# Half of the softmax maxima move from a matmul into eight biased exponentials, and small Newton steps move from VectorE to GpSimd, in a cross-attention and six-layer local-attention kernel

## The chip, the cores and the metric

The kernel runs on one core of a Trainium2 chip. A core has a matmul engine (TensorE, PE in the profile; its weight loads are listed apart as PEld), VectorE (DVE), ScalarE (ACT), GpSimd (POOL), a queue that only issues transfers (SyncE, SP), and DMA engines that carry them out. Each engine works through its own list of instructions in order and waits on semaphores where another engine's result is needed. The metric is the device time of one execution in microseconds; lower is better.

## The reference

The input is 32 sequences of 128 tokens of width 128. First comes one cross-attention block (16 heads of width 8, 4 key and value heads), then six layers that each hold a local attention and a feed-forward block. What matters here is the local attention of one layer:

```python
q, k, v = split(shift_tokens(x) @ Wqkv)            # 16 heads of width 64
q = q / max(norm(q), 1e-12) * q_scale              # the same for k
q, k = rotary(q), rotary(k)
# windows of 32 queries, each against its own and the window before it: 64 keys
sim  = einsum('bhwie,bhwje->bhwij', q, look(k)) * 8.0
sim  = where(mask, -big, sim)
attn = softmax(sim, -1)                            # a row of 64 keys
x    = (einsum('bhwij,bhwje->bhwie', attn, look(v))) @ Wo + x
```

The feed-forward block after it is a layer norm, two projections to 341 columns with a GELU gate, and a projection back. All of it is computed in fp32, with most weights split into a high and a low part for the fast fp32 format of TensorE.

## The kernel before, in words

The 32 sequences form 8 groups of 4. After the cross-attention (`xgroup`, `xunit`) the kernel loops over 6 layers and 8 groups, 48 times `lgroup`. Each calls `unit` four times, once per sequence, and then `ffn`. So there are 192 units, and nearly all of the time goes into them.

One unit, with the operation's name in the planner and its line in the profile:

- `qk` (L437 to L439): four projections of 512 columns, each as three matmuls; `sq` (L785, ACT) squares them, `ss` (L800, DVE) sums the squares per head; `tab` (L791, DVE) multiplies with the rotary tables; `add` (L797, POOL) adds the two rotary parts.
- `newton` turns the 32 sums of squares per token into inverse norms, exp(-0.5 ln v) and one Newton step. For the units' norms (`floor` is given) `dmx` (L395) clamps on VectorE, `ln` and `ep` (L398, L401) and the square `ysq` (L405) run on ScalarE, and two fused steps `dnw` (L411, L417) run on VectorE. For the layer norms (`eps` is given, 4 values per token) the same function runs on GpSimd in five small steps (L393, L407, L413, L419, L422).
- `mul` (L814, POOL) applies the inverse norms, `tq` (L443, PE) transposes, `evq` (L819, ACT) copies out of PSUM.
- `msk` (L856, ACT) writes the mask into the two score banks (bank 66 for the even heads, a = 0, bank 67 for the odd heads, a = 1); `sc` (L851, PE) adds the scores, 128 small matmuls.
- `soft(a)`, for each bank: `mx` (L864, DVE) takes minus the maximum of each of eight rows of 64 scores; `fold` (L865, PE) adds it to the scores in PSUM, a matmul of the identity with the maxima broadcast to 512 columns; `ex` (L867, ACT) is one exponential over 512 columns; `sm` and `rl` (L868, L869, DVE) sum and invert, `pl` (L870, POOL) normalizes, `pt` (L872, DVE) transposes in blocks of 32.
- `y`, `yt`, `dm` (L437 to L439, L832 ACT, L833 SP) make the values and move them with a transfer; `av` (L885, PE) sums over keys.

Each engine's order is not the program's order. Every operation is handed to a scheduler, `Sched`, with a priority (the unit's number plus an offset in the table `LATER`) and with costs in the table `COST` (engine, time on it, time until done). `Sched.run` plays these through and fixes the order in which the instructions are written for each engine; `KEEP` says how many PSUM banks of the five common ones an operation must leave free. The chip then follows that order, whatever its own durations are. Units overlap deeply: while the scores of unit u run, the projections of units u+3 and u+4 and the norms of u+2 are under way.

`ffn` per group: `res` (L893, DVE) adds the attention, `psh` (L750 and L751, SP) shifts tokens by a transfer, `st` (L899, DVE) takes statistics after it, `xn` (L913, ACT) normalizes in four pieces with a scale and a bias from SBUF, `gate` and `pa` (PE), `gel` (L930, ACT, with a bias from SBUF and a change of ScalarE's table before and after), `um` (DVE), `w2` (L949, PE).

Of the kernel before, what the change touches and what calls it, by code (L numbers as in the profile page):

```python
# [16 lines left out]
P = 128  # L17
# [4 lines left out]
GB = 4  # L22
TX = 0.44
NS = 4
NW = "dve"


COST = dict(
    ax=("PE", 0.4, 0.64), axh=("ACT", 0.52, 0.62), axl=("DVE", 0.6, 0.7),
    qk=("PE", 0.75, 0.95), sq=("ACT", 0.52, 0.62), ss=("DVE", .62, .72), tab=("DVE", 1.14, 1.22), add=("POOL", 1.28, 1.31), ta=("DVE", .63, .72), adda=("POOL", 1.1, 6),  # L30
    mxs=("POOL", .26, .30), dmx=("DVE", 0.4, 0.48), dnw=("DVE", 0.34, 0.42), ln=("ACT", .2, .24), ep=("ACT", .2, .24), nw=("POOL", .31, .34),
    mul=("POOL", 1.01, 1.06), tq=("PE", 0.44, 0.68), evq=("ACT", .5, .62), evk=("ACT", .5, .62),
    y=("PE", 0.75, 0.95), yt=("ACT", 0.52, 0.62), dm=("SP", 0.6, 8.0), xph=("ACT", .6, .7), xpl=("ACT", .6, .7), dw=("SP", .62, 3.5), dr=("SP", .62, 4.5),
    msk=("ACT", 0.54, 0.63), sc0=("PE", .52, .75), sc1=("PE", .52, .75), mx=("DVE", .62, .7), fold=("PE", 0.31, 0.5), ex=("ACT", .5, .62),
    sm=("DVE", .62, .7), rl=("DVE", .14, .22), pl=("POOL", 1.05, 1.07), pt=("DVE", .64, .74), av=("PE", 1.95, 2.15), sc=("PE", 1.42, 1.62),
    res=("DVE", .63, .72), psh=("SP", 1.65, 3.5), st=("DVE", 0.78, 0.86), ag=("DVE", .35, .40), xn1=("POOL", 1.08, 1.1),
    eps=("POOL", .22, .26), lnf=("ACT", .22, .21), epf=("ACT", .22, .21), nwf=("POOL", 0.18, 0.24), xn=("ACT", 1.55, 1.65), nmr=("DVE", 0.4, 0.48), ysq=("ACT", .2, .24), xn2=("POOL", 1.08, 1.1),
    ptn=("PE", .46, .70), xnh=("ACT", .51, .62), xnl=("DVE", .60, .66), gate=("PE", 0.75, 0.95), gel=("ACT", 0.63, 0.7),
    pa=("PE", 0.73, 0.94), um=("DVE", 0.68, 0.76), w2=("PE", .67, .90), res2=("DVE", .63, .72), xo=("POOL", 1.3, 1.3),
# [4 lines left out]
    xst=("DVE", 0.8, 0.87), xag=("DVE", .30, .35), xnw=("POOL", .20, .20), xtr=("PE", 0.52, 0.68), xev=("ACT", .49, .60),  # L44
    xpj=("PE", 0.98, 1.15), hil=("ACT", .58, .70), lof=("DVE", .66, .75), pv=("PE", .90, 1.1), vt=("DVE", .25, .30),
    td=("PE", .90, 1.1), abs=("ACT", .52, .65), lnb=("ACT", .55, .64), mkb=("DVE", .42, .42), tbm=("DVE", .95, 1.0),
    xsc=("PE", 0.38, 0.58), xmx=("DVE", .86, .95), xsb=("POOL", 1.10, 1.10), xex=("ACT", .55, .65), xpa=("PE", 1.1, 1.3),
    xrl=("DVE", 0.17, 0.25), xat=("DVE", .21, .29), pwm=("PE", .90, 1.1), xrs=("DVE", .63, .70),
)

LATER = dict(y=2.95, fold=4, xsc=-0.75, evk=-0.25, ss=0.5, sq=4.05, axl=-2.3, mul=1.5, mx=-0.75, evq1=0.1, tab0=-2.0,
    lnb=0.75, xpj=0.85, tab3=0.85, lnf=0.45, dmx=-0.5, xst=1.05, tq3=2.45, xat=0.7, pv=1.9, msk0=-2.15, sq2=-0.65,
    nw=1.5, pa2=-0.85, xex=3.7, lof=-0.25, ss1=1.1, xmx=-1.85, yt0=-1.3, mul3=0.55, io=-0.85, rl0=4.05, bip=-1.45,
    td=0.25, add3=4.1, gate0=-1.55, add0=-2.5, xnh=-0.95, ex1=-0.4, pa0=1.6, pl0=3.1, bid=3.5, ln=0.95, ss2=-0.75,
    sq0=0.25, sq1=0.35, xpa=0.25, qkl=3, mul0=-2, xn1=4.1, tq2=-0.25, mul1=1.45, xsb=1.7, w2=-2.0, sq3=0.5, ex=-0.5,
    wvp=-1.05, ax=-0.5, xtr=0.1, qk3=-1.65, qk=-0.7, evq0=0.65, qkh=1.0, w1b=-0.6, pl1=2.8, mh=3, yt3=0.5, gel2=-1.65,
    w1a=0.95, tab2=-0.25, ysq=-1.05, qk1=-2.15, res=2.2, xo=0.25, av=0.75, tq1=1.0, epf=-1.3, gate2=-1.75, pa1=4,
    tab=0.35, mx1=-0.5, sm0=1.85, pt0=-0.05, gel0=-1.05, ml=-1.5, ptn=2.1, ep=-2.75, sm1=-0.65, xrl=-1.4, um=1,
    add2=3, dm=-1, evq=0.45, tq0=1.3, nwf=3, yt1=-1.1, msk=-1.5, um2=-1.6, pwm=-0.2, w1c=0.1, mkb=0.95, gel=0.95,
    pt1=-0.75, wve=2.25, fold1=-0.75, gate=0.75, xnl=-0.1, dm3=-2.25, xn=4.2, yt2=-0.75, st=-0.5, xag=0.5, mul2=1.75,  # L60
    tb=-1, psh=-0.25, rl1=2.1, pl=1.75, yt=-0.75, evq3=1, dnw=-1, um1=0.45, sm=-0.25, abs=0.6, gate1=0.3, msk1=-0.05,
    dm0=0.6, gel1=-0.4, nmr=2.0, fold0=-2.5, axh=-0.75, y3=3.1, res2=2.75, dm2=0.5, vt=2, hil=-1.3, ss0=0.5, pa=1.5,
    eps=-1, dm1=0.45, xev=0.45, um0=-1, ag=0.75, tq=0.25)

KEEP = dict(qk=0, y=0, gate=1, pa=1, xtr=0, xpj=0, pv=1, td=1, xsc=1, wvp=2, mp=2, bip=2, sc0=0, tq=0, ptn=0, ax=0,
    w2=1)
LAT = dict(PE=.06, ACT=.05, DVE=.08, POOL=.16, SP=.08)


# [156 lines left out]
def body(ctx: ExitStack, tc: tile.TileContext, x, ctx_in, fside, mask_in, xWq, xWk, xWv, xWo, xtw,  # L226
         Wqkv, q_scale, k_scale, Wo, ln_g, ln_b, W1, b1, W2, b2, cst, x1d, out):
    nc = tc.nc
# [153 lines left out]
    def newton(names, pri, V, src, n, floor, eps, pool_, cols):  # L382
        v, y, t = [Buf(p) for p in pool_]

        def sl(b):
            return b.t[:, 0:n]

        small = NW == "dve" and floor is not None
        e = nc.vector if small else nc.gpsimd

        def f0():
            if eps is not None:
                e.tensor_scalar(sl(v), cols(), eps, None, op0=ALU.add)  # L393
            else:
                e.tensor_scalar(sl(v), cols(), floor, None, op0=ALU.max)  # L395

        def f1():
            nc.scalar.activation(sl(y), sl(v), AF.Ln)  # L398

        def f2():  # L400
            nc.scalar.activation(sl(y), sl(y), AF.Exp, scale=-0.5)  # L401

        def f3():
            if small:
                nc.scalar.activation(sl(t), sl(y), AF.Square)  # L405
            else:
                e.tensor_tensor(sl(t), sl(y), sl(y), op=ALU.mult)  # L407

        def f4():
            if small:  # L410
                e.scalar_tensor_tensor(sl(t), sl(v), -0.5, sl(t), op0=ALU.mult, op1=ALU.mult)  # L411
            else:
                e.tensor_tensor(sl(t), sl(t), sl(v), op=ALU.mult)  # L413

        def f5():
            if small:
                e.scalar_tensor_tensor(sl(y), sl(t), 1.5, sl(y), op0=ALU.add, op1=ALU.mult)  # L417
            else:
                e.tensor_scalar(sl(t), sl(t), -0.5, 1.5, op0=ALU.mult, op1=ALU.add)  # L419
# [6 lines left out]
        S.op("ysq" if small else names[3], f3, pri, [y], [t])  # L426
        S.op(names[3], f4, pri, [t, v], [t])
        if small:
            S.op(names[3], f5, pri, [y, t], [y])
        else:  # L430
            S.op(names[3], f5, pri, [t], [t])
            S.op(names[3], f6, pri, [y, t], [y])
        return y

    def split3(pt, lhs, rhs):
# [336 lines left out]
    def unit(l, g, j, w, G, pri):  # L772
# [29 lines left out]
            S.op("add", add, pri, [t], [rt], k=c)  # L802
        for c in range(4):
            proj(c)
        rn = newton(("dmx", "ln", "ep", "dnw") if NW == "dve" else ("mxs", "ln", "ep", "nw"), pri, None, ss, 32, 1e-24, None, ("rv", "ry", "rw"), lambda: ss.t)
        qT = []
        for c in range(4):
            def tr(c):
# [50 lines left out]
        def r8(b):  # L859
            return b.t.rearrange("p (a c) -> p a c", c=64)  # L860

        def soft(a):
            s, mx, pr, sm, PT = sc[a], Buf("mx"), Buf("pr"), Buf("sm"), PTs[a]
            S.op("mx", lambda: nc.vector.tensor_reduce(mx.t, r8(s), axis=AX.X, op=ALU.max, negate=True), pri, [s], [mx], k=a)  # L864
            S.op("fold", lambda: nc.tensor.matmul(s.t, identr, mx.t.unsqueeze(2).to_broadcast([P, 8, 64]), start=False,  # L865
                                                  stop=True, skip_group_check=True), pri, [mx, s], [s], k=a)
            S.op("ex", lambda: nc.scalar.activation(pr.t, s.t, AF.Exp), pri, [s], [pr], table="E", k=a)  # L867
# [168 lines left out]
```

## Time and profile before

| | |
|---|---|
| time, median of 3 runs | 3084.66 us (3080.82 to 3087.93) |
| the profiled execution's own time | 3085.37 us |
| its span, first to last instruction | 3083.6 us |
| mean granted TensorE clock | 0.987 |
| busy: PE, DVE, POOL, ACT | 96%, 90%, 78%, 76% of the span |
| instructions | 114504 |

A line of the profile names the source line, engine, operation, and output tile <- input tiles. "Busy" is the time in which at least one instruction of that engine ran, by the profile. The ends of matmuls are modelled and include the way into PSUM, so that two following matmuls overlap in the list; the distance from one start to the next says what a matmul costs on the engine. The windows view gives busy times per stretch with the number of instructions in brackets. The chain is the sequence of work that ended last, followed backwards from the end of the program.

### The profile page before, as it was taken

Reading aid. Unit: us, or ns where it says so; the run is one execution under the profiler, and the core shown is the slowest. Engines: PE = TensorE matmul, PEld = TensorE weight load, DVE = VectorE, ACT = ScalarE, POOL = GpSimd, SP = SyncE. Lnnn points to the kernel's source line nnn. Section 1 sums busy time; section 2 is a strip of 40 time slices with the busy share of each in tenths; the row PEclk is TensorE's granted clock in tenths of the full one; section 3 lists DMA queues with packets and bytes.
Section 4 is the critical chain, followed back from the end, with each engine's and each line's share of the span. In section 5 each row is a group of like instructions: output and inputs, shape, how many; then the busy total and the mean of one; then the engine's idle time right before and its main releaser. Section 6 shows DMA issues by size and latency. Waiting matters only on the chain.

```text
span 3083.6 us, 114504 instructions
## 1 busy us (share of the span) xinstructions
PE 2960.5 (96%) x47887; PEld 2337.7 (76%) x47887; DVE 2787.6 (90%) x5779; ACT 2335.2 (76%) x4799; POOL 2416.5 (78%) x2470
## 2 busy tenths in 40 slices
PE   8999999999999999999999999999999999999997
PEld 5666777787777777777777777777777787777785
DVE  5778999998999999999999999999999998999994
ACT  6877777777777777777777777777777877777774
POOL 6667978878878878878878878878788787778783
PEclk7999999999999999999999999999999999999998
DMA  4100645545544546544446544446545455445454
GB/s 111 32 17 22 102 74 82 89 74 94 95 75 79 89 78 104 92 76 82 85 76 105 90 79 83 80 80 106 87 77 87 74 89 92 78 88 88 83 92 67
DMA packets 216870, 250.70 MB, mean 81 GB/s; under 512 B 90622, under 2 KB 111394, under 8 KB 216354
## 3 DMA queue, kind: packets, MB, share of 16 engines
q1 hardware_dynamic: 215922, 243.04, 45.5%
q8 instruction: 377, 6.18, 1.1%
q14 instruction: 139, 1.14, 0.2%
q10 hardware_dynamic: 432, 0.34, 0.0%
HBM read 25.31 MB, written 4.19 MB: 10 GB/s over the span
## 4 chain that ended last, share of the span: by engine, by line
PE 55%; DVE 27%; ACT 7%; DMA 5%; issue 5%; SPq 1%; POOL 0%; DVEq 0%; POOLq 0%; ACTq 0%
PE bank__68 L885 8%; DMA xt<-xt 4%; PE bank__66 L851 2%; PE bank__65 L443 2%; PE bank__62 L443 2%; PE bank__64 L443 2%; PE bank__62 L949 2%; PE bank__63 L437 2%; PE bank__67 L851 2%; PE bank__65 L437 2%; PE bank__64 L437 2%; PE bank__61 L437 2%; PE bank__63 L443 2%; PE bank__63 L439 2%; PE bank__63 L438 2%
## 5 line engine op out<-in xcount | busy, mean ns | idle before, releaser
L856 ACT COPY bank__66<-mask 128x512 f32<-128x512 f32 x192 | 117.3, 611 | 4.7 <-PE bank__66 L361 4.7
L856 ACT COPY bank__67<-mask 128x512 f32<-128x512 f32 x192 | 115.5, 602 | 1.7 <-PE bank__67 L361 0.7
L244 ACT ACT_TABLE_LOAD x48 | 61.6, 1283 | 0.9
L930 ACT ACT_TABLE_LOAD x48 | 61.6, 1283 | 0.8
L722 ACT ACTIVATE ysh__88<-ysh__88 128x512 f32<-128x512 f32 x64 | 40.4, 640 | 5.1 <-POOL ysh__88 L720 4.9
L893 DVE TENSOR_TENSOR xt<-bank__68,xt 128x512 f32<-128x512 f32 x48 | 32.6, 679 | 1.2 <-PE bank__68 L885 1.2
L953 DVE TENSOR_TENSOR xt<-bank__62,xt 128x512 f32<-128x512 f32 x25 | 16.3, 653 | 2.8 <-PE bank__62 L949 2.8
L960 POOL TENSOR_TENSOR raw__49499<-raw__49499,xt 128x512 f32<-128x512 f32 x1 | 1.3, 1261 | 14.9 <-DVE xt L953 14.9
L870 POOL TENSOR_TENSOR pr__50308<-pr__50308,sm__50312 128x512 f32<-128x512 f32 x1 | 1.0, 1042 | 14.4 <-DVE sm__50317 L869 14.4
L725 ACT COPY ysh__88<-bank__63 128x512 f32<-128x512 f32 x13 | 7.7, 592 | 5.7 <-PE bank__63 L443 5.6
L443 PE MATMUL bank__64<-cs,ysh__88 128*128 128x128 f32 x56 | 9.8, 302 | 2.2 <-ACT ysh__88 L722 1.6
L725 ACT COPY ysh__88<-bank__61 128x512 f32<-128x512 f32 x15 | 8.9, 592 | 2.9 <-PE bank__61 L443 2.6
L443 PE MATMUL bank__61<-cs,ysh__88 128*128 128x128 f32 x60 | 10.8, 309 | 0.3 <-ACT ysh__88 L722 0.3
L693 DVE TENSOR_TENSOR xt<-bank__68,xt 128x512 f32<-128x512 f32 x8 | 5.5, 685 | 6.1 <-PE bank__68 L691 6.1
L722 ACT ACTIVATE wch__92<-wch__92 128x512 f32<-128x512 f32 x16 | 10.3, 644 | 0.6 <-POOL wch__92 L720 0.6
L722 ACT ACTIVATE wch__91<-wch__91 128x512 f32<-128x512 f32 x16 | 10.2, 636 | 0.7 <-POOL wch__91 L720 0.7
L722 ACT ACTIVATE wch__89<-wch__89 128x512 f32<-128x512 f32 x16 | 10.1, 632 | 0.3 <-POOL wch__89 L720 0.3
L443 PE MATMUL bank__63<-cs,ysh__88 128*128 128x128 f32 x52 | 9.7, 316 | 0.6 <-ACT ysh__88 L722 0.6
L722 ACT ACTIVATE wch__90<-wch__90 128x512 f32<-128x512 f32 x16 | 10.1, 632 | 0.2 <-POOL wch__90 L720 0.2
L725 ACT COPY ysh__88<-bank__64 128x512 f32<-128x512 f32 x14 | 8.3, 594 | 2.5 <-PE bank__64 L443 2.4
L443 PEld LDWEIGHTS bank__61<-cs,ysh__88 128*128 128x128 f32 x60 | 8.0, 159 | 2.8 <-DVE rt__2246 L635 0.8
L443 PEld LDWEIGHTS bank__64<-cs,ysh__88 128*128 128x128 f32 x56 | 6.7, 152 | 4.2 <-ACT ysh__88 L722 1.7
(25307 smaller groups left out, 15502.2 us busy)
## 6 DMA issues: line engine op xcount, KB each, us to landing
xt<-xt SPq DMA_DIRECT2D x96, 112.0 KB
xt<-in_x SPq DMA_DIRECT2D x16, 128.0 KB
x_scratch<-xt SPq DMA_DIRECT2D x8, 256.0 KB
xt<-xt SPq DMA_DIRECT2D x96, 15.0 KB
stg__828<-in_L_ffn_Wo SPq DMA_DIRECT2D x1, 512.0 KB
stg__5116<-in_L_ffn_Wo SPq DMA_DIRECT2D x1, 512.0 KB
stg__18724<-in_L_ffn_Wo SPq DMA_DIRECT2D x1, 512.0 KB
stg__26543<-in_L_ffn_Wo SPq DMA_DIRECT2D x1, 512.0 KB
```

What stands on the lines that cost most here:

```text
L244: S.back = lambda: nc.scalar.preload_act_table_set("natural_log_exp_and_others")
L437: nc.tensor.matmul(pt, lh, rh, start=True, stop=False)
L438: nc.tensor.matmul(pt, lh, rl, start=False, stop=False)
L439: nc.tensor.matmul(pt, ll, rh, start=False, stop=True)
L443: nc.tensor.transpose(dst[:, k * P:(k + 1) * P], srcs[k], ident if eye is None else eye)
L722: S.op("xex", lambda: nc.scalar.activation(sm.t, sm.t, AF.Exp), pri, [sm], [sm], table="E")
L851: nc.tensor.matmul(s4[a][32 * c:32 * c + 32, half, wd, lo:64], q[r, c * P + 32 * wd:c * P + 32 * wd + 32], k[r, c * P + 32 * wd - 32 + lo: ...
L856: S.op("msk", lambda b=b: nc.scalar.copy(b.t, mask), pri, (), [b], k=a)
L885: nc.tensor.matmul(po.t[32 * wd:32 * wd + 32, j * P:(j + 1) * P], p5[a][:, half, wd, blk, :], ysh[0].t[:, u * 512 + h * P:u * 512 + (h + 1 ...
L893: S.op("res", lambda: nc.vector.tensor_tensor(xv(g), hv(po.t), xv(g), op=ALU.add), pri, [po, X[g]], [X[g]])
L930: S.op("gel", lambda: nc.scalar.activation(u.t[0:n], pg.t[0:n], AF.Gelu, bias=b1c.t[0:n, 1, i:i + 1]), pri, [pg, b1c], [u], table="G", k=i)
L949: nc.tensor.matmul(py.t[:, k * P:(k + 1) * P], us_[i].t[0:r_, k * P:(k + 1) * P], w2t.t[0:r_, i, :], start=(i == 0), stop=(i == 2))
```

## The change

For the even heads' bank (a = 0) the matmul `fold` and the single exponential `ex` go. In their place `exb` runs eight exponentials of 64 columns on ScalarE, each with one column of `mx` as its bias per partition. The odd heads' bank keeps `fold` and `ex`.

In `newton`, the steps for the units' norms move from VectorE to GpSimd: one clamp (`mxs`, in place of `dmx`) and three small steps (`nw`, in place of the two fused `dnw`). The square stays on ScalarE.

The tables `COST`, `LATER` and `KEEP` have new values, so the order of all engines is drawn up anew. Transfers are the same ones in another order.

```diff
+FOLD = (1,)
...
-    mxs=("POOL", .26, .30), dmx=("DVE", 0.4, 0.48), dnw=("DVE", 0.34, 0.42), ... nw=("POOL", .31, .34),
+    mxs=("POOL", 0.2, 0.26), dmx=("DVE", 0.4, 0.48), dnw=("DVE", 0.34, 0.42), ... nw=("POOL", 0.18, 0.24),
...
+    ... exb=("ACT", 1.6, 1.7),
...
-LATER = dict(y=2.95, fold=4, xsc=-0.75, ...
+LATER = dict(y=0.25, xsc=-0.15, evk=-0.25, ...
...
-KEEP = dict(qk=0, y=0, gate=1, pa=1, xtr=0, xpj=0, pv=1, td=1, xsc=1, ..., ptn=0, ax=0, w2=1)
+KEEP = dict(qk=0, y=0, gate=0, pa=1, xtr=0, xpj=1, pv=1, td=1, xsc=0, ..., ptn=1, ax=1, w2=2)
...
-        small = NW == "dve" and floor is not None
-        e = nc.vector if small else nc.gpsimd
+        e = nc.gpsimd
+        big = floor is not None
...
         def f4():
-            if small:
-                e.scalar_tensor_tensor(sl(t), sl(v), -0.5, sl(t), op0=ALU.mult, op1=ALU.mult)
-            else:
-                e.tensor_tensor(sl(t), sl(t), sl(v), op=ALU.mult)
+            e.tensor_tensor(sl(t), sl(t), sl(v), op=ALU.mult)
         def f5():
-            if small:
-                e.scalar_tensor_tensor(sl(y), sl(t), 1.5, sl(y), op0=ALU.add, op1=ALU.mult)
-            else:
-                e.tensor_scalar(sl(t), sl(t), -0.5, 1.5, op0=ALU.mult, op1=ALU.add)
+            e.tensor_scalar(sl(t), sl(t), -0.5, 1.5, op0=ALU.mult, op1=ALU.add)
         def f6():
             e.tensor_tensor(sl(y), sl(y), sl(t), op=ALU.mult)
...
-            S.op("fold", lambda: nc.tensor.matmul(s.t, identr, mx.t.unsqueeze(2).to_broadcast([P, 8, 64]), ...
-            S.op("ex", lambda: nc.scalar.activation(pr.t, s.t, AF.Exp), pri, [s], [pr], table="E", k=a)
+            if a in FOLD:
+                S.op("fold", ...
+                S.op("ex", ...
+            else:
+                def pieces():
+                    for i in range(8):
+                        nc.scalar.activation(r8(pr)[:, i], r8(s)[:, i], AF.Exp, bias=mx.t[:, i:i + 1].bitcast(F32))
+                S.op("exb", pieces, pri, [mx, s], [pr], table="E", k=a)
```

More of the change, by code (lines that the diff above doesn't have):

```diff
@@ L24 @@
 NS = 4
-NW = "dve"
+FOLD = (1,)
 COST = dict(
     ax=("PE", 0.4, 0.64), axh=("ACT", 0.52, 0.62), axl=("DVE", 0.6, 0.7),
[L30 to L35, printed above, removed]
+    qk=("PE", 0.75, 0.95), sq=("ACT", 0.53, 0.63), ss=("DVE", 0.6, 0.68), tab=("DVE", 1.14, 1.22), add=("POOL", 1.27, 1.3), ta=("DVE", .63, .72), adda=("POOL", 1.1, 6),
+    mxs=("POOL", 0.2, 0.26), dmx=("DVE", 0.4, 0.48), dnw=("DVE", 0.34, 0.42), ln=("ACT", .2, .24), ep=("ACT", .2, .24), nw=("POOL", 0.18, 0.24),
+    mul=("POOL", 1.01, 1.06), tq=("PE", 0.44, 0.68), evq=("ACT", 0.51, 0.61), evk=("ACT", .5, .62),
+    y=("PE", 0.75, 0.95), yt=("ACT", 0.52, 0.62), dm=("SP", 0.58, 7.0), xph=("ACT", .6, .7), xpl=("ACT", .6, .7), dw=("SP", .62, 3.5), dr=("SP", .62, 4.5),
+    msk=("ACT", 0.54, 0.63), sc0=("PE", .52, .75), sc1=("PE", .52, .75), mx=("DVE", 0.6, 0.68), fold=("PE", 0.31, 0.5), ex=("ACT", .51, .62), exb=("ACT", 1.6, 1.7),
+    sm=("DVE", 0.6, 0.68), rl=("DVE", 0.13, 0.21), pl=("POOL", 1.02, 1.06), pt=("DVE", 0.62, 0.7), av=("PE", 1.95, 2.15), sc=("PE", 1.45, 1.65),
     res=("DVE", .63, .72), psh=("SP", 1.65, 3.5), st=("DVE", 0.78, 0.86), ag=("DVE", .35, .40), xn1=("POOL", 1.08, 1.1),
@@ L43 @@
     mp=("PE", 0.5, 0.7), mh=("ACT", .28, .38), ml=("DVE", .33, .42),
-    xst=("DVE", 0.8, 0.87), xag=("DVE", .30, .35), xnw=("POOL", .20, .20), xtr=("PE", 0.52, 0.68), xev=("ACT", .49, .60),
+    xst=("DVE", 0.8, 0.87), xag=("DVE", .30, .35), xnw=("POOL", .20, .20), xtr=("PE", 0.54, 0.68), xev=("ACT", .49, .60),
     xpj=("PE", 0.98, 1.15), hil=("ACT", .58, .70), lof=("DVE", .66, .75), pv=("PE", .90, 1.1), vt=("DVE", .25, .30),
     td=("PE", .90, 1.1), abs=("ACT", .52, .65), lnb=("ACT", .55, .64), mkb=("DVE", .42, .42), tbm=("DVE", .95, 1.0),
-    xsc=("PE", 0.38, 0.58), xmx=("DVE", .86, .95), xsb=("POOL", 1.10, 1.10), xex=("ACT", .55, .65), xpa=("PE", 1.1, 1.3),
+    xsc=("PE", 0.4, 0.58), xmx=("DVE", .86, .95), xsb=("POOL", 1.04, 1.07), xex=("ACT", .55, .65), xpa=("PE", 1.1, 1.3),
@@ L48 @@
     xrl=("DVE", 0.17, 0.25), xat=("DVE", .21, .29), pwm=("PE", .90, 1.1), xrs=("DVE", .63, .70),
 )
[L51 to L63, printed above, removed]
@@ L65 @@
-KEEP = dict(qk=0, y=0, gate=1, pa=1, xtr=0, xpj=0, pv=1, td=1, xsc=1, wvp=2, mp=2, bip=2, sc0=0, tq=0, ptn=0, ax=0,
-    w2=1)
+LATER = dict(y=0.25, xsc=-0.15, evk=-0.25, axl=-2, tab0=-2.1, xpj=-0.05, tq3=2.8, pv=2.0, sq2=-0.25, nw=1.9, xex=3.65,
+    ss1=0.45, mul3=-0.3, rl0=4.35, bip=-1.6, add3=1, pl0=3.8, bid=-0.35, ss2=-0.65, sq1=-0.95, xpa=0.35, tq2=1.6,
+    w2=-1.55, mx0=1, sq3=0.15, wvp=2.4, ax=-0.15, qk3=-0.35, qk=-1.35, yt3=1.0, tab2=-1.45, ysq=-0.85, tq1=0.65,
+    gate2=-3.4, mx1=-0.5, um=1, add2=1.9, dm=-0.3, w1c=0.7, fold1=0.25, gate=-2.95, xn=-1.5, st=1.45, mul2=2,
+    dnw=-1.1, fold0=-2.5, y3=3.15, dm1=-1.2, ag=0.6, ss3=-0.2, exb0=5.25, axh=-0.25, y2=1.95, mp=1.95, eps=2.35,
+    pl1=4.05, add0=5.8, xat=-1.3, xst=1.15, tq0=-2.45, nwf=1.5, pt1=1.55, lnf=1.7, io=-1.5, xrs=1.9, msk1=-1.5,
+    msk0=1.25, xn1=1.5, ss=-1.5, um0=1.5, ex1=0.25, y1=3.55, sq0=-0.75, pwm=-0.1, evq0=1.1, vt=-0.55, qkl=2, xo=1.65,
+    add1=0.1, mul0=0.75, abs=2.55, mkb=2.8, qk1=-0.7, pa2=-3.0, qkh=1.1, mxs=-0.95, psh=-1.45, um2=-0.25, yt0=1.0,
+    res=3, yt1=-0.7, tab1=0.4, av=1.4, td=2.9, gel0=0.75, evq1=-1.55, lnb=-2, evq2=-0.7, ep=0.55, pt=-1.45, xnh=0.1,
+    evq3=0.5, ss0=3.1, ldw=-2, add=-2.0, yt=4.4, um1=0.25, y0=2.9, xmx=0.2, gel=0.8, ml=1.5, gate1=-0.75, epf=3.05,
+    xrl=-1.5, exb=1.95, pa0=0.95, xsb=-0.4, xnl=-1, nmr=-0.25, mul=0.1, gel2=-0.8, mul1=-0.8, fold=-0.75, wve=1.4,
+    rl=-2.15, res2=2.9, hil=4.0, pl=-1.0, tab=0.85, xn2=-0.8, ptn=2.5, sc=1.5, w1a=2, mx=3.9, w1b=-0.7, sm=0.3,
+    gel1=1.0, gate0=0.25, msk=3, tb=-0.25, sm1=-0.25, pt0=-0.5, pa=3.95, rl1=-0.5, evq=-0.5, mh=-1, sq=0.75, dm2=2.5,
+    dm3=4, xag=0.25)
@@ L67 @@
+KEEP = dict(qk=0, y=0, gate=0, pa=1, xtr=0, xpj=1, pv=1, td=1, xsc=0, wvp=2, mp=2, bip=2, sc0=0, tq=0, ptn=1, ax=1,
+    w2=2)
 LAT = dict(PE=.06, ACT=.05, DVE=.08, POOL=.16, SP=.08)
@@ L403, in f3 @@
         def f3():
-            if small:
+            if big:
                 nc.scalar.activation(sl(t), sl(y), AF.Square)
@@ L409, in f4 @@
         def f4():
-            if small:
-                e.scalar_tensor_tensor(sl(t), sl(v), -0.5, sl(t), op0=ALU.mult, op1=ALU.mult)
-            else:
-                e.tensor_tensor(sl(t), sl(t), sl(v), op=ALU.mult)
+            e.tensor_tensor(sl(t), sl(t), sl(v), op=ALU.mult)
         def f5():
-            if small:
-                e.scalar_tensor_tensor(sl(y), sl(t), 1.5, sl(y), op0=ALU.add, op1=ALU.mult)
-            else:
-                e.tensor_scalar(sl(t), sl(t), -0.5, 1.5, op0=ALU.mult, op1=ALU.add)
+            e.tensor_scalar(sl(t), sl(t), -0.5, 1.5, op0=ALU.mult, op1=ALU.add)
         def f6():
@@ L425, in newton @@
         S.op(names[2], f2, pri, [y], [y], table="E")
-        S.op("ysq" if small else names[3], f3, pri, [y], [t])
+        S.op("ysq" if big else names[3], f3, pri, [y], [t])
         S.op(names[3], f4, pri, [t, v], [t])
[L428 to L432, printed above, removed]
+        S.op(names[3], f5, pri, [t], [t])
+        S.op(names[3], f6, pri, [y, t], [y])
         return y
@@ L804, in unit @@
             proj(c)
-        rn = newton(("dmx", "ln", "ep", "dnw") if NW == "dve" else ("mxs", "ln", "ep", "nw"), pri, None, ss, 32, 1e-24, None, ("rv", "ry", "rw"), lambda: ss.t)
+        rn = newton(("mxs", "ln", "ep", "nw"), pri, None, ss, 32, 1e-24, None, ("rv", "ry", "rw"), lambda: ss.t)
         qT = []
@@ L864, in soft @@
             S.op("mx", lambda: nc.vector.tensor_reduce(mx.t, r8(s), axis=AX.X, op=ALU.max, negate=True), pri, [s], [mx], k=a)
-            S.op("fold", lambda: nc.tensor.matmul(s.t, identr, mx.t.unsqueeze(2).to_broadcast([P, 8, 64]), start=False,
-                                                  stop=True, skip_group_check=True), pri, [mx, s], [s], k=a)
-            S.op("ex", lambda: nc.scalar.activation(pr.t, s.t, AF.Exp), pri, [s], [pr], table="E", k=a)
+            if a in FOLD:
+                S.op("fold", lambda: nc.tensor.matmul(s.t, identr, mx.t.unsqueeze(2).to_broadcast([P, 8, 64]), start=False,
+                                                      stop=True, skip_group_check=True), pri, [mx, s], [s], k=a)
+                S.op("ex", lambda: nc.scalar.activation(pr.t, s.t, AF.Exp), pri, [s], [pr], table="E", k=a)
+            else:
[3 more added lines that the diff above has]
+                S.op("exb", pieces, pri, [mx, s], [pr], table="E", k=a)
             S.op("sm", lambda: nc.vector.tensor_reduce(sm.t, r8(pr), axis=AX.X, op=ALU.add), pri, [pr], [sm], k=a)
```

## The prediction

> **What bounds the kernel now.** I read the page's busy shares first, then its chain of waits, then the windows view of a steady stretch, 1400 to 2600 us, in which 83 units run (the two folds count 166).
>
> ```profile
> PE 2960.5 (96%) x47887; PEld 2337.7 (76%) x47887; DVE 2787.6 (90%) x5779; ACT 2335.2 (76%) x4799; POOL 2416.5 (78%) x2470
> ...
> PE 55%; DVE 27%; ACT 7%; DMA 5%; issue 5%; SPq 1%; POOL 0%; DVEq 0%; POOLq 0%; ACTq 0%
> ```
>
> ```profile
> 1400.00:2600.00 1200.00, 1165.23 (x20020) 933.24 (x20018) 1125.84 (x1953) 923.33 (x1904) 967.99 (x960) 1.00 0.50 86
> ```
>
> The five times after the comma are PE, PEld, DVE, ACT and POOL. PE is 97% and DVE 94% busy; ACT has 23% and POOL 19% idle. The chain passes between PE and DVE: 55% and 27%. So PE sets the pace with DVE close behind, and ACT and POOL are the cover. The change takes work from the first two and gives it to the last two. Next, what the touched operations cost there (windows view again, in turn: the folds L865 with PE and PEld, then L395, L411 and L417 on DVE).
>
> ```profile
> 1400.00:2600.00 1200.00, 75.43 (x166) 30.97 (x166) 1.00 0.50 86
> ...
> 1400.00:2600.00 1200.00, 33.22 (x83) 1.00 0.50 86
> ...
> 1400.00:2600.00 1200.00, 38.86 (x83) 1.00 0.50 86
> ...
> 1400.00:2600.00 1200.00, 29.59 (x84) 1.00 0.50 86
> ```
>
> The three Newton steps on DVE have only 32 columns and still cost 0.40, 0.47 and 0.35 us. The timeline shows why:
>
> ```profile
> 1499.21 1.04 POOL L814 TENSOR_TENSOR rt__23585<-rt__23585,ry__23927 128x512 f32<-128x512 f32 x1
> 1499.61 0.69 DVE L411 SCALAR_TENSOR_TENSOR rw__24070<-rv__23993,rw__24070 128x32 f32<-128x32 f32 x1
> 1500.21 1.28 POOL L797 TENSOR_TENSOR rt__23984<-t__24065 128x512 f32<-128x512 f32 x1
> 1500.82 0.72 DVE L417 SCALAR_TENSOR_TENSOR ry__24061<-rw__24070,ry__24061 128x32 f32<-128x32 f32 x1
> ```
>
> L411 ends at 1500.30, just after the GpSimd operation that ended at 1500.25; L417 ends at 1501.54, after the one that ended at 1501.49. Elsewhere the same L411 takes 0.18 us. A small VectorE step that begins beside a large GpSimd step lasts until that one is over. Last, who PE waits for (waits view of the same stretch):
>
> ```profile
> PE bank__66 L865 <- DVE mx__26487 L864: 2.1, 1, 2.1
> PE bank__66 L865 <- DVE mx__42119 L864: 2.1, 1, 2.1
> PE bank__66 L865 <- DVE mx__23601 L864: 1.3, 1, 1.3
> ```
>
> Bank 66 is the even heads' fold, the one that goes. Over the whole run 48 rows of this form are listed; they add to 38.6 us. None for bank 67 is among the 200 longest.
>
> **Part by part.** I cost against the profiled execution, 3085.4 us (3083.6 of span and 1.8 around it), which is 0.7 us over the median of 3084.7.
>
> The even fold on PE. Its price is the distance to the next matmul:
>
> ```profile
> 1510.64 0.48 PE L865 MATMUL bank__66<-mx__24294,identr 128*128 128x512 f32 x1
> 1510.96 0.60 PE L443 MATMUL bank__63<-cs,rt__23701 128*128 128x128 f32 x4
> ```
>
> That is 0.32 us. The chain gives 0.22 where matmuls follow each other tightly, the busy time gives 75.43/166 = 0.45, the way into PSUM included. I take 0.32: 192 x 0.32 = 61 us, between 42 and 87. PE is on the path, so this counts in full. Its wait goes with it: 39 us. What is late next is the odd fold. In the order before, the even fold of a group's last unit has only y1 and tq0 between it and the scores (0.70 + 0.44 = 1.1 us of PE work, three matmuls of 0.23 and four of 0.11 in the chain). In the new order the odd fold has between qk2, y1, tq0, tq1 (2.3 us, third unit) and pa1, tq0, av and four w2 (5.7 us, last unit). DVE needs two maxima of 0.60 us in that time, so I expect little of the wait to come back: 0, at most the 39 us.
>
> The Newton steps on DVE. 33.2 + 38.9 + 29.6 = 101.7 us of 1125.8 go, 9.0% of its work, 1.22 us per unit. On the chain DVE has 27%, 833 us; 9% of that is 75 us. Much is the same time as the fold's wait, since a late maximum is how a late DVE reaches PE. I add 10 us beyond the 39, between 0 and 36 (75 - 39).
>
> The eight exponentials on ACT. The rows nearest (source view of L663, then timeline of the two ex of a unit):
>
> ```profile
> L663 ACT ACTIVATE rt__140<-bank__61,nct x4: 359/367/376, 10.3 to 11.1; 128x128 f32<-128x128 f32 x4
> ```
>
> ```profile
> 1527.34 0.60 ACT L867 ACTIVATE pr__24591<-bank__66 128x512 f32<-128x512 f32 x1
> 1527.83 0.60 ACT L867 ACTIVATE pr__24598<-bank__67 128x512 f32<-128x512 f32 x1
> ```
>
> L663 reads PSUM with a bias from SBUF, 128 columns; its four take 1.14 us in the timeline, so they follow at (1.14 - 0.367)/3 = 0.258 us. A column costs 0.83 ns (L930, 512 columns with a bias, 686 ns; L663 367 ns; 319/384). With 64 columns fewer a piece follows at 0.205 us, eight at 1.64, where ex takes 0.49. Extra: 1.15 us per unit, 221 us in all. Bounds: 0 (pieces no dearer than the whole) and 8 x 0.258 - 0.49 = 1.57 us. ACT goes from 923.3/83 = 11.1 to 12.3 us of the 14.5 a unit now takes: covered on average. But the list is in order: behind exb stand ex1, evq2, msk0 and msk1 of the same and the next unit, and PE's sc waits for the masks and the copied q and k. The chain has 7% on ACT, 216 us; if that grows with the work by 1.15/11.1 = 10%, it costs 22 us. Without the cover it is the 221.
>
> Here a rule speaks against the change. The Trainium skill, "ScalarE: Activation LUTs", section "What ACT_TABLE_LOAD costs", gives an ACTIVATE with a bias pointer a fixed part of 280 ns plus 0.833 ns per column, and 93 ns of overlap between neighbours. That is an estimate of 240 ns per piece and 1.92 us for eight, 0.28 us per unit more than the rows give; by it the chain term would be 28 us instead of 22. The column price agrees with the 0.83 above.
>
> The small steps on POOL. The trace shows them with 4 columns:
>
> ```profile
> 1527.05 0.20 POOL L407 TENSOR_TENSOR nw__24585<-ny__24576 128x4 f32<-128x4 f32 x1 [0.82 <-ACT ny__24576 L401]
> 1527.33 0.20 POOL L413 TENSOR_TENSOR nw__24585<-nw__24585,nv__24567 128x4 f32<-128x4 f32 x1
> 1527.62 0.19 POOL L419 TENSOR_SCALAR nw__24585<-nw__24585 128x4 f32<-128x4 f32 x1
> ```
>
> Steps that need each other follow at 0.28 us. With 0.22 for the clamp (L393) and 2 ns per added column (L814: 1.04 us for 512), four come to about 1.05 us per unit, between 0.6 (0.15 each) and 1.4; 202 us in all. POOL rises from 968/83 = 11.7 to 12.7 us per unit. The cover is its idle 19%, and 0% of the chain lies on it, so 0; if the cover is gone, up to the 202 us.
>
> The new order. Transfers are the same in number. Between res and st, which waits for the shift's transfer, DVE has six operations in either order: 4.3 us before, 4.1 after, by the busy times of their kinds. 48 x 0.2 = 10 us of DVE waiting at most, off the path if PE has work; 0. The cross-attention (the first 345 us) keeps its operations; I count no difference, within 10 us.
>
> Sum: 61 + 39 + 10 - 22 = 88 us less than 3085.4, so 2997; 2995 with the 0.7 to the median, rounded.
>
> **The rivals.**
>
> Larger gain, 2940. DVE, not PE, is the true pace. For it: 27% of the chain. Then the whole 75 us count beside the fold's 61 and 39 and the 22 of ACT: 153 us. PE's idle between 345 and 3000 us is 2655 - 2576 = 79 us, so 61 + 79 = 140 is about the most PE can return. Both lead to 2930 to 2950.
>
> The waits move, 3055. The even fold's 39 us come back at the odd fold or at av, which now hears from exb later by 1.15 us. What stays is the fold's occupancy of 42 to 61 us less 22: 3047 to 3066. Against it: the longer distance to the fold in the new order.
>
> ScalarE becomes the bound: slower. Place: exb and the copies queued behind it. Price: up to 1.15 us per unit, 221 us, against the 61 + 39 + 10 = 110 gained; it decides once over half of the extra time reaches PE. With 75% it is 166 - 110 = +56: 3140; with all, 3196. For it: four engines would then all be near 12.3 to 13 us per unit, and every pause of one reaches the others. Against it: 23% idle ScalarE and 7% of the chain.
>
> That the change doesn't do what it says is out: the built program has 192 folds, 1536 pieces and 768 more small GpSimd steps.
>
> **How the numbers follow.** Forecast 0.50 (2960 to 3035), larger gain 0.15, waits move 0.15, ScalarE 0.16, and 0.04 for an end within 0.2% (6 us, about what a measurement here can tell from no change). Faster: 0.50 + 0.15 + 0.15 = 0.80; same 0.04; slower 0.16. The range takes in the first three cases and the even one, 2935 to 3080; outside lie the slower case and a little of the larger gain.
>
> **What would show it.** Right: rows of L411 and L417 gone from DVE, its busy share down by about 6 points to 84%; hardly any PE wait on mx; ACT and POOL at 85% or more; eight pieces in about 1.75 us. Wrong: PE waits on msk, evq or exb rows that add to over 100 us (ScalarE), rows of bank 67's fold with waits of 1 us (waits move), or a chain with POOL in it.

## The result, and the profile after

The change makes the kernel slower: 3119.6 us, median of five runs (3113.21 to 3125.27), against 3085.0 (3080.82 to 3097.4) in the five runs beside them. The ratio is 1.0105, interval 1.0082 to 1.0128, or 25 to 39 us in 3085 us; the forecast was 2995. The profiled execution took 3125.27 us (span 3123.5, clock 0.986 against 0.987 before), 40 us over the profiled one of before.

The page's busy shares and chain after the change:

```profile
PE 2932.2 (94%) x47695; PEld 2302.2 (74%) x47695; DVE 2599.8 (83%) x5203; ACT 2511.7 (80%) x6143; POOL 2595.8 (83%) x3238
...
PE 46%; DVE 22%; ACT 13%; issue 8%; POOL 6%; DMA 4%; SPq 0%; POOLq 0%; DVEq 0%; ACTq 0%
```

The work went where it was said to go: PE lost 28 us of busy time, DVE 188, while ACT gained 177 and POOL 179. Yet the span grew by 40 us. No engine is now as busy as PE was; PE and DVE are idle for more of the time. On the chain PE went from 55% to 46%, ACT from 7% to 13%, issue from 5% to 8%, and POOL from 0% to 6%.

The windows view of 1400 to 2600 us, first all work, then the eight exponentials alone (L865), then the odd folds alone (L859, on PE and PEld):

```profile
1400.00:2600.00 1200.00, 1144.89 (x19641) 914.07 (x19636) 1032.02 (x1674) 985.54 (x2445) 1031.22 (x1273) 0.99 0.56 84
...
1400.00:2600.00 1200.00, 145.04 (x657) 0.99 0.56 84
...
1400.00:2600.00 1200.00, 36.26 (x82) 15.72 (x82) 0.99 0.56 84
```

82 units run in this stretch instead of 83; PE is 95% busy instead of 97%, DVE 86% instead of 94%. DVE, ACT and POOL are now all between 82% and 86%.

The waits view of PE in the same stretch, four of its longest rows:

```profile
PE bank__68 L884 <- issue: 9.6, 11, 2.8
PE bank__67 L859 <- DVE mx__37289 L857: 4.4, 1, 4.4
...
PE bank__67 L844 <- ACT bank__67 L849: 3.2, 12, 0.3
PE bank__61 L430 <- ACT sq__27834 L778: 1.9, 1, 1.9
```

The fold waits for its maximum again, now in bank 67 and for up to 4.4 us, though VectorE has 8 points less to do. Over 345 to 3000 us (this stretch is used for all sums of waits below, of waits over 0.15 us where nothing else is said) PE waited 69 us before: 39 for DVE, 12 for ACT, 18 for issue, 1 for POOL. After the change it is 144: 45 for DVE, 48 for ACT, 39 for issue, 10 for transfers and 3 for POOL. Over the whole span PE is idle for 191 us instead of 123: 68 us more idle time against 28 us less work makes the 40 lost.

The units' mask copies into bank 66 show where. From that of the 5th unit to that of the 33rd the kernel takes 432 us instead of 404, and from there to the last unit's 1.6% more. At the second unit it is 10 us ahead (301 us against 310), but so are exb_in_place, pieces_only and newton_pool_in_place (described below), whose changes set in only shortly before it (at 265 us or later). The granted clock of the first 345 us was 0.93 in the profile of before and 0.96 to 0.98 in these four, so these 10 us are not counted for the change.

### The profile page after: what moved, and what is told of

It reads as the page before. It is cut to its first block, busy times and chain, and to the rows that moved or that the text cites. A ratio compares the mean times of both kernels' runs of the same rounds, so it can differ in the third digit from the quotient of the medians.

```text
span 3123.5 us, 115512 instructions
## 1 busy us (share of the span) xinstructions
PE 2932.2 (94%) x47695; PEld 2302.2 (74%) x47695; DVE 2599.8 (83%) x5203; ACT 2511.7 (80%) x6143; POOL 2595.8 (83%) x3238
## 4 chain that ended last, share of the span: by engine, by line
PE 46%; DVE 22%; ACT 13%; issue 8%; POOL 6%; DMA 4%; SPq 0%; POOLq 0%; DVEq 0%; ACTq 0%
PE bank__68 L884 7%; DMA xt<-xt 2%; PE bank__63 L436 2%; PE bank__66 L844 2%; PE bank__61 L430 2%; PE bank__65 L430 2%; PE bank__64 L430 2%; PE bank__65 L436 2%; PE bank__64 L436 2%; PE bank__61 L436 2%; PE bank__62 L430 1%; PE bank__62 L436 1%; PE bank__63 L430 1%; PE bank__67 L844 1%; PE bank__65 L431 1%
## 5 line engine op out<-in xcount | busy, mean ns | idle before, releaser
L849 ACT COPY bank__66<-mask 128x512 f32<-128x512 f32 x192 | 125.4, 653 | 5.9 <-DMA xt<-in_x 4.9
L849 ACT COPY bank__67<-mask 128x512 f32<-128x512 f32 x192 | 125.6, 654 | 1.1 <-PE bank__67 L363 1.1
L959 POOL TENSOR_TENSOR raw__50872<-raw__50872,xt 128x512 f32<-128x512 f32 x1 | 1.3, 1260 | 13.6 <-DVE xt L952 13.6
L436 PE MATMUL bank__63<-cs,ysh__88 128*128 128x128 f32 x60 | 10.1, 294 | 0.4 <-ACT xh__1332 L758 0.2
L436 PEld LDWEIGHTS bank__63<-cs,ysh__88 128*128 128x128 f32 x60 | 6.8, 146 | 4.8 <-issue 2.3
L436 PE MATMUL bank__62<-cs,ysh__88 128*128 128x128 f32 x52 | 9.2, 304 | 0.6 <-ACT ysh__88 L715 0.6
L718 ACT COPY ysh__88<-bank__63 128x512 f32<-128x512 f32 x15 | 8.9, 593 | 0.6 <-PE bank__63 L436 0.6
L436 PE MATMUL bank__64<-cs,xt 128*128 128x128 f32 x60 | 9.3, 277 | 0.0
```

What stands on the lines that cost most here:

```text
L436: nc.tensor.transpose(dst[:, k * P:(k + 1) * P], srcs[k], ident if eye is None else eye)
L718: S.op("xev", lambda: nc.scalar.copy(sm.t, pt.t), pri, [pt, sm], [sm])
L849: S.op("msk", lambda b=b: nc.scalar.copy(b.t, mask), pri, (), [b], k=a)
```

## The experiments

Two theories were set against each other at first. **The work**: removing the fold gives less than counted and the pieces cost more than counted, wherever they stand. **The order**: the work is as forecast, and the new order costs what the work gains. "In place" below means that each engine keeps the instruction order of before: the planner's tables and operations are those of before, and only what an operation issues differs.

**The tables alone, the work alone.** Four kernels: the work of before in an order drawn from the new tables, and the new work in the old order, in two halves and together.

```diff
 # old_work_new_tables
+COST, LATER, KEEP = those of after          # folds, ex and newton as before
 # exb_in_place
-            S.op("fold", lambda: nc.tensor.matmul(...), pri, [mx, s], [s], k=a)
-            S.op("ex", lambda: nc.scalar.activation(pr.t, s.t, AF.Exp), ...)
+            if a == 0:                               # else: fold and ex as before
+                S.op("fold", lambda: None, ...)      # planned, not issued
+                S.op("ex", pieces, ...)              # eight of 64 columns, where ex stood
 # newton_pool_in_place                              # planned as dmx and dnw, issued on GpSimd
-                e.tensor_scalar(sl(v), cols(), floor, None, op0=ALU.max)
+                nc.gpsimd.tensor_scalar(sl(v), cols(), floor, None, op0=ALU.max)
-                e.scalar_tensor_tensor(sl(t), sl(v), -0.5, sl(t), ...)
+                nc.gpsimd.tensor_tensor(sl(t), sl(t), sl(v), op=ALU.mult)
-                e.scalar_tensor_tensor(sl(y), sl(t), 1.5, sl(y), ...)
+                nc.gpsimd.tensor_scalar(sl(t), sl(t), -0.5, 1.5, ...)
+                nc.gpsimd.tensor_tensor(sl(y), sl(y), sl(t), op=ALU.mult)
 # both_in_place: the last two together
```

> The kernel before with the cost, offset and bank tables of the kernel after: two folds, Newton on VectorE, only the order is new. Theory 'order' (the order drawn from the new tables is worse whatever work it carries): 3120 us or more. Theory 'ScalarE' (the eight pieces sit in ScalarE's list and make what stands behind them late) and theory 'GpSimd' (the small steps come late from GpSimd's list): near the 3085 us of before, within 20 us, since neither cause is in it.

> The order of the kernel before, kept instruction by instruction; only the even fold is not issued and the eight pieces stand where the even exponential stood. Theory 'order': the fold's 61 us and its 39 us of waiting are saved and 22 us of ScalarE come back, 2990 to 3030 us. Theory 'ScalarE': slower than before, 3100 to 3170 us (half or more of the 221 us of extra ScalarE time comes through). Theory 'GpSimd': as 'order', 2990 to 3030 us.

> The order of the kernel before; only the three Newton steps of the units' norms are issued on GpSimd (four steps) at the same places, both folds stay. Theory 'order' and theory 'ScalarE': VectorE is relieved of 1.2 us per unit, 3030 to 3070 us. Theory 'GpSimd': the inverse norms come late and the 202 us of added GpSimd time come through by a third or more, 3120 us or more.

> The whole of the new work in the order of the kernel before: pieces where the even exponential stood, no even fold, Newton on GpSimd at the old places. Theory 'order': 2960 to 3020 us, what was predicted for the change. Theory 'ScalarE': 3090 to 3160 us. Theory 'GpSimd': 3090 us or more, and well above the run with the pieces alone.

Measured: old_work_new_tables 3188.3 us, ratio 1.0340 (1.0292 to 1.0388). exb_in_place 3162.5, 1.0257 (1.0209 to 1.0305). newton_pool_in_place 3068.8, 0.9954 (0.9931 to 0.9978). both_in_place 3171.7, 1.0287 (1.0242 to 1.0332).

Both theories hold a part. (For both_in_place the theory 'ScalarE' had said 3160 us at most; it came out 12 us above.) The new work in the old order costs 89 us, and all of it comes with the even heads' half; the Newton half alone gains 14 us. The redrawn order gives back 1.0287 - 1.0105 = 1.8%, 56 us, with the new work, and costs 105 us with the old. So new tables are not good or bad by themselves.

What the pieces do is seen in the timeline of exb_in_place, ScalarE and PE:

```profile
1616.64 1.77 ACT L868 ACTIVATE pr__26277<-bank__66,mx__26254 128x64 f32<-128x64 f32 x8
1618.22 0.66 ACT L819 COPY qT__26267<-bank__62 128x512 f32<-128x512 f32 x1
```

```profile
1617.01 0.60 PE L443 MATMUL bank__64<-cs,rt__25824 128*128 128x128 f32 x4
1618.93 0.50 PE L437 MATMUL bank__62<-wch__18662,xh__25690 128*128 128x512 f32 x1 [1.33 <-ACT qT__26267 L819]
```

The copy of the transposed q out of bank 62 (`evq`, L819) stands behind the pieces. Until it is done, bank 62 is not free, and PE's next projection waits 1.33 us for that bank. PE's waits for ACT rise from 12 us to 58 in this kernel, 47 of them at L437 for that copy. Its waits for VectorE rise too, from 39 us to 107, most of them at the odd fold (93 us); in fold_out_only below the odd fold waits 81 us without any pieces, so most of this part is not theirs.

**The fold and the pieces apart.** Two kernels in the old order and two in the new one.

```diff
 # fold_out_only (order of before)
+            if a == 0:                               # else: fold and ex as before
+                S.op("fold", lambda: None, ...)
+                S.op("ex", lambda: nc.scalar.activation(pr.t, s.t, AF.Exp), pri, [mx, s], ...)
 # pieces_only (order of before; both folds stay)
+                    for i in range(8):
+                        nc.scalar.activation(r8(pr)[:, i], r8(s)[:, i], AF.Exp, bias=zero)
 # after_one_exp (order of after)
-                    for i in range(8):
-                        nc.scalar.activation(r8(pr)[:, i], ..., bias=mx.t[:, i:i + 1].bitcast(F32))
+                    nc.scalar.activation(pr.t, s.t, AF.Exp, bias=mx.t[:, 0:1].bitcast(F32))
 # after_newton_dve (order of after): the clamp and the two fused steps issued on VectorE,
 # where the order has the four GpSimd steps
```

> The order of the kernel before; the even fold is not issued and the even heads keep one exponential, without their maximum subtracted (that part is left out). ScalarE's work is that of before. Theory 'fold pays' (the sum of the prediction): 61 + 39 us saved, 2985 us, at least 3020. Theory 'wait inherited' (the odd fold stands right behind and waits for the later maximum, so the even fold ran inside that wait): 3050 to 3085 us, and the waits of the odd fold on VectorE's maxima rise from a few us to 60 us or more.

> The order of the kernel before; both folds stay, and the even exponential is eight pieces of 64 columns with a column of zeros as bias. Only ScalarE's work grows, by about 1.25 us per unit. Theory 'ScalarE' (what stands behind the pieces is late for PE): slower by 60 to 120 us, 3140 to 3200 us, with PE waiting on the copies of q and k. Theory 'covered' (the 22 us of the prediction): 3100 us or less.

> The order of the kernel after; the eight pieces are one exponential of 512 columns with the first column of the maxima as bias for all even heads (seven of eight maxima are left out). Theory 'ScalarE': the time the pieces take comes back, 3000 to 3060 us. Theory 'order' (the new order keeps engines waiting for other reasons): 3090 us or more.

> The order of the kernel after; the Newton steps of the units' norms are issued on VectorE again (a clamp and two fused steps) at the new places. If moving them to GpSimd is worth its small gain in this order too: 3125 to 3160 us. Theory 'GpSimd' (the steps are late from GpSimd's list in the new order): 3100 us or less.

Measured: fold_out_only 3077.8 us, 0.9992 (0.9971 to 1.0013). pieces_only 3181.8, 1.0326 (1.0295 to 1.0357). after_one_exp 3091.6, 1.0028 (1.0009 to 1.0047). after_newton_dve 3179.5, 1.0317 (1.0283 to 1.0352).

In the old order, taking 192 matmuls off the busiest engine gains nothing that can be measured. The page's shares of fold_out_only and the two longest rows of a fold among the waits of PE between 1400 and 2600 us:

```profile
PE 2920.4 (95%) x47695; PEld 2310.3 (75%) x47695; DVE 2780.1 (90%) x5779; ACT 2331.6 (76%) x4799; POOL 2416.4 (78%) x2470
```

```profile
PE bank__67 L869 <- DVE mx__26401 L864: 3.4, 1, 3.4
PE bank__67 L869 <- DVE mx__41969 L864: 2.8, 1, 2.8
```

PE is 40 us less busy, and the waits of folds for maxima grew from 36.5 us (45 rows) to 81.4 (88 rows), 45 us more. The wait did not go with the even fold; it went to the odd one, and took the even fold's own time with it. The trace of before has a reason in rows that the prediction didn't read, among the weight loads:

```profile
1526.55 0.19 PEld L865 LDWEIGHTS bank__66<-mx__24564,identr 128*128 128x128 f32 x1 [0.59 <-DVE mx__24564 L864]
1527.15 0.19 PEld L865 LDWEIGHTS bank__67<-mx__24571,identr 128*128 128x128 f32 x1 [0.41 <-DVE mx__24571 L864]
```

Here the odd fold stands directly behind the even one and waits 0.41 us more for its own maximum, which VectorE makes after the even one. The even fold ran inside that time. In the list of matmuls this wait is hidden, since the even fold's modelled end (0.48 us) covers most of it. Among the weight loads of before, between 345 and 3000 us, the odd fold has 59 waits of 0.2 us or more, 24 us in all, beside the even one's 84 with 66 us; in fold_out_only the odd one has 100 with 120 us.

But the two folds are neighbours in only 71 of the 192 units; in most of the others four transposes or one projection stand between them. Over the whole run the weight loads of folds wait 89 us for maxima instead of 69 in the 71 units, and 40 us instead of 25 in the 121 others. So the fold that ran inside a wait is seen in some 60 units. In the others PE, having less to do, comes to the odd fold earlier and waits there for VectorE.

pieces_only shows the price of the pieces without any other edit: 100 us in the old order. Its chain:

```profile
PE 42%; ACT 23%; DVE 22%; issue 6%; DMA 5%; POOL 2%; SPq 1%; DVEq 0%; POOLq 0%; ACTq 0%
```

and a row of PE's waits between 1400 and 2600 us:

```profile
PE bank__64 L439 <- ACT qT__28451 L821: 1.2, 1, 1.2
```

ACT has 23% of the chain instead of 7%, and PE's projections wait 57 us for the copies of q and k (3 before). In the order of after the same pieces cost far less: after_one_exp, which lacks only them, is at 1.0028, so they cost 1.0105 - 1.0028 = 0.8% there, 24 us. PE waits for these copies are 12 us in after (L430 behind L812). But after_one_exp is also no faster than before, though it has neither the even fold nor the pieces nor the Newton steps on DVE. Its shares and its chain, and then two rows of PE's waits between 1400 and 2600 us (here L883 is `av`):

```profile
PE 2912.7 (94%) x47695; PEld 2297.3 (74%) x47695; DVE 2608.6 (84%) x5203; ACT 2337.6 (76%) x4799; POOL 2594.6 (84%) x3238
...
PE 62%; DVE 15%; ACT 7%; issue 6%; DMA 5%; POOL 5%; SPq 0%; POOLq 0%; DVEq 0%; ACTq 0%
```

```profile
PE bank__68 L883 <- issue: 7.9, 9, 2.7
PE bank__67 L859 <- DVE mx__36358 L857: 4.4, 1, 4.4
```

after_newton_dve says that in the new order the GpSimd steps are worth 1.0317 - 1.0105 = 2.1%, 65 us, over four times what they are worth in the old one; that order was planned with them on GpSimd. I had expected 3125 to 3160 us, so this gain was larger than I thought.

**What remained: do the parts add up, and what does redrawing do?** A further theory was that PE and DVE take turns in setting the pace, so that fold and Newton steps gain only together.

```diff
 # fold_out_newton_pool: fold_out_only and newton_pool_in_place together (order of before)
 # newton_split_in_place: newton_pool_in_place, but the clamp stays on VectorE; both folds
-                nc.gpsimd.tensor_scalar(sl(v), cols(), floor, None, op0=ALU.max)
+                e.tensor_scalar(sl(v), cols(), floor, None, op0=ALU.max)
 # newton_pool_replanned: work of newton_pool_in_place, planned as mxs and nw, order drawn anew
+    mxs=("POOL", 0.28, 0.34), nw=("POOL", 0.21, 0.25),     # LATER and KEEP of before
 # new_work_old_tables: the whole work of after, order drawn anew
+    exb=("ACT", 1.6, 1.7), mxs=..., nw=...                 # LATER and KEEP of before; exb=-0.5, as ex had
```

> The order of the kernel before; the even fold is not issued, the even heads keep one exponential without their maximum subtracted (left out), and the Newton steps are issued on GpSimd: the change without its extra ScalarE work. Theory 'alternating pace' (PE and VectorE hold each other up, so that relief of one alone shows little and relief of both shows much): 3040 us or less. Theory 'order' (in a fixed order each engine waits for the places given to the others, whoever has less to do): about the sum of the two single edits, 3055 to 3075 us.

> The order of the kernel before; the clamp stays on VectorE and only the steps after the square are issued on GpSimd. In the run with all steps on GpSimd, ScalarE waited 142 us in all for the clamp from GpSimd's list. Theory 'late clamp': without that wait 3030 to 3060 us. Theory 'not on the path': 3065 to 3080 us, as with all steps moved.

> The Newton part alone, with the order drawn anew by the scheduler from the offsets of the kernel before and GpSimd's costs (0.28 and 0.21 us for the small steps). Theory 'a new drawing fits the work': 3040 us or less, better than the same steps in the old order (3069). Theory 'offsets and work belong together' (a drawing with offsets made for other work costs by itself): 3100 us or more.

> The whole new work, its order drawn from the offsets and bank table of the kernel before, with the pieces at 1.6 us. Theory 'offsets and work belong together': slower than the kernel after (3120) by 20 us or more, 3140 to 3200 us. Theory 'the new offsets are worse in themselves': 3100 us or less.

Measured: fold_out_newton_pool 3067.6 us, 0.9951 (0.9930 to 0.9972). newton_split_in_place 3058.5, 0.9912 (0.9889 to 0.9934). newton_pool_replanned 3124.9, 1.0128 (1.0103 to 1.0153). new_work_old_tables 3108.4, 1.0073 (1.0048 to 1.0098).

The theory of turns falls: 0.9951 is what the two parts give by themselves (0.9992 x 0.9954 = 0.9946). My expectation for new_work_old_tables, 3140 to 3200 us, was missed as well. I had thought that the new offsets and the new work belong together; but with the old offsets and a price for the pieces in the planner the redrawn order is as good as that of after (the intervals 1.0048 to 1.0098 and 1.0082 to 1.0128 overlap). So the offsets of after are not needed to cover most of the pieces' cost. That the planner's knowing their length does it is likely, but not shown: no run draws the order anew with the length left as it was. newton_pool_replanned shows the reverse: the same work that gains 14 us in the old order loses 39 us when the order is drawn anew with the old offsets, a swing of 54 us for the order alone. Under their new names the moved steps also take other offsets from the old table (1.5 for `nw` where `dnw` had -1, none for `mxs` where `dmx` had -0.5); whether the loss comes from these or from the rest of the drawing, no run separates.

newton_split_in_place computes all that the reference asks for and beats both kernels: 27 us under before, about 60 under the change (0.9912 against 1.0105). Its shares and chain:

```profile
PE 2951.6 (97%) x47887; PEld 2339.1 (77%) x47887; DVE 2679.0 (88%) x5395; ACT 2330.2 (76%) x4799; POOL 2535.6 (83%) x3046
...
PE 55%; DVE 21%; POOL 7%; ACT 7%; issue 5%; DMA 4%; SPq 1%; DVEq 0%; POOLq 0%; ACTq 0%
```

With the clamp on GpSimd too, the logarithm `ln` waits on ScalarE for it, as a row of ACT's waits in newton_pool_in_place shows (1400 to 2600 us):

```profile
ACT ry__38372 L398 <- POOL rv__38365 L395: 2.8, 1, 2.8
```

The clamp stands in GpSimd's list behind operations of over 1 us, and everything behind `ln` on ScalarE waits with it: 142 us in 93 rows. In newton_split_in_place there is no such row, ACT's waits for VectorE's clamp are 81 us (98 in before), and POOL's share of the chain is 7% where newton_pool_in_place has 16%.

## Why the prediction was wrong

The sum was -61 (fold) - 39 (its wait) - 10 (Newton steps) + 22 (pieces) + 0 (order) = -88. In ratios to before the runs give, one step after the other: fold out 0.9992 (-2 us); with the Newton steps 0.9951 (-13); in the order of after 1.0028 (+24); with the pieces 1.0105 (+24). That is -2 - 13 + 24 + 24 = +33 us, the 1.05% measured. The shares depend on the sequence: with the pieces put in ahead of the new order, they cost 104 us and the new order gives 56 back. The forecast of each step is set against it here.

**The fold and its wait, 61 + 39 us: the step that failed.** About 2 us were paid (interval: 9 gained to 4 lost). The working priced the fold by the distance to the next matmul and counted it in full, with "PE is on the path". But a matmul that stands ahead of a wait isn't on the path, even on an engine that is 96% busy: the odd fold, soon behind the even one in PE's list, waits for a later maximum of the same unit. In fold_out_only PE had 40 us less work and 45 us more waits of folds. No run puts the even fold back into the order of after, so what it is worth there is not measured. The prediction looked only for waits at bank 67 in the list of matmuls and found none among the longest. (Of its 48 rows of 38.6 us one, of 0.7 us, is a wait for a copy by ScalarE, not for a maximum.) The "waits move" rival named the right place, the odd fold, but let the occupancy of 42 to 61 us stand and so gave 3055; the wait took that too. The argument against it, the longer distance to the fold in the new order, didn't hold: after the change the odd fold still waits 32 us, up to 4.4 in one place.

**The Newton steps, 10 us: right in size.** 14 us in the old order. The bound of 36 us stood as well: with the clamp left where it was, they give 27. That a clamp on GpSimd holds up ScalarE's `ln` wasn't priced; POOL was put at 0 because nothing on the chain lay on it, which the moved work changed.

**The pieces, 22 us: right in size in the order of after (24), but only there.** In the old order they cost 100 us (pieces_only), 82 (exb_in_place against fold_out_only) or 104 (both_in_place against fold_out_newton_pool), 37% to 47% of the 221 us of extra ScalarE time. So the rival "ScalarE becomes the bound" had its place right, exb and the copies queued behind it. Its condition, over half of the extra time, was not reached; less was enough, since the 110 us of gain set against it were mostly missing. Its remark that four engines would be near 12.3 to 13 us per unit doesn't come out for PE, which by 1165 us for 83 units, less one fold, is at 13.6 to 13.7. The estimate by chain share (7% of the chain, grown by a tenth) says nothing about what stands behind a longer operation; that it came out near the measured 24 is not shown to be more than luck.

**The new order, 0 us: the second step that failed.** At nearly equal work (fold out, Newton steps on GpSimd, one exponential) the order of after costs 1.0028 - 0.9951 = 0.8%, 24 us, against that of before. The work differs in one thing: the single exponential of after_one_exp has a bias from SBUF and takes 0.58 us to the next start instead of 0.49, 18 us of ScalarE time over the run. The prediction looked at transfers and at one stretch between `res` and `st`, and took the rest as neutral. The runs show that an order drawn anew is worth tens of us, up to 105, in either direction: -56 for the new work, +54 for the Newton steps alone, +105 for the old work. What in the order of after costs those 24 us is not settled. From fold_out_newton_pool to after_one_exp PE's waits rise from 103 to 139 us: those at `av` from 2 to 33 (13 on issue, 13 on transfers, 7 on DVE) and those for banks held until `sq` has read them from 0 to 31, while those of the odd fold for its maximum fall from 50 to 28. No run took one of these away, so this is argued only.

**What was to show it.** Eight pieces in 1.75 us, DVE at 84%: seen (1.75 and 83%). ACT and POOL at 85%: 80% and 83% over the span, 82% and 86% in the stretch. "Hardly any PE wait on mx" was wrong. Of the signs of failure, long waits at bank 67's fold and a chain with POOL in it were seen; over 100 us of PE waits on ACT were not (48). The range was said to take in the even case as well, but an end within 6 us of 3085 lies almost wholly above its 3080.

## What to carry to other kernels

Before an operation is credited with its own time, look at what stands behind it in its engine's list, in the weight loads as well as the matmuls: if the next one, or one soon after it, waits for a later result of the same producer, removing the first can buy nothing until the producer is earlier. An operation made longer on an engine with idle time costs by what is queued behind it, here above all the copies that free PSUM banks; let the planner know its length, though no run here shows what that alone is worth. When a change comes with a newly drawn order, price the order by itself, by running the new work in the old one: here the fastest version measured was a small edit, three of four small steps moved and nothing redrawn.

## What the runs showed of the hardware

The pieces follow each other faster than was estimated. In the timeline of after, eight of them and, for comparison, the single exponential of the odd heads:

```profile
1502.56 1.75 ACT L865 ACTIVATE pr__24211<-bank__66,mx__24167 128x64 f32<-128x64 f32 x8
1504.60 0.69 ACT L861 ACTIVATE pr__24258<-bank__67 128x512 f32<-128x512 f32 x1
```

Over the 192 units eight take 1.765 us on average, from the start of the first to the listed end of the last. From start to start it is 0.197 us, 1.58 us for eight; the prediction had 0.205 and 1.64 from the rows. The Trainium skill, "ScalarE: Activation LUTs", section "What ACT_TABLE_LOAD costs", led to an estimate of 0.240 and 1.92 us; the measurement decides for the smaller one.

What the prediction read from two rows of VectorE holds over the whole run of before: of the 123 clamps (L395) that begin beside a GpSimd operation of over 0.8 us, 122 end within 0.12 us of its end, and the 123 take 0.58 us on average; the 69 others take 0.16.

The small steps on GpSimd with 32 columns cost as the 4-column ones had suggested, in the timeline of after:

```profile
1526.85 0.25 POOL L412 TENSOR_TENSOR rw__24648<-rw__24648,rv__24513 128x32 f32<-128x32 f32 x1
...
1527.48 0.25 POOL L418 TENSOR_TENSOR ry__24550<-ry__24550,rw__24648 128x32 f32<-128x32 f32 x1
```

With the clamp (0.285 us on average) the four make 1.01 us per unit, where 1.05 was worked out.

One thing was not expected and stays open: ScalarE's other operations are listed longer where pieces run. The mask copy, in the page's groups of after:

```profile
L849 ACT COPY bank__66<-mask 128x512 f32<-128x512 f32 x192 | 125.4, 653 | 5.9 <-DMA xt<-in_x 4.9
```

takes 653 ns here, 664 in exb_in_place and 667 in pieces_only, but 611 to 613 in before and in fold_out_only, newton_pool_in_place and after_one_exp, which have none. The median distance from its start to the next start stays at 516 to 519 ns in all seven, so the longer listing costs ScalarE hardly any time of its own.
